# A table of 41 ranks for TensorE's order, and first-tile scores on quarters of the array

## The chip, the core and the metric

The kernel runs on one NeuronCore of a Trainium2 chip. Its time is the device time of one execution in microseconds; a comparison uses the median of several runs. TensorE (PE) multiplies matrices, VectorE (DVE), ScalarE (ACT) and GpSimd (POOL) do the rest, SyncE (SP) issues the transfers. All data are 32-bit floats.

## What is computed

Eight sequences of 512 tokens with 256 features. Each is layer-normalised and goes two ways. One is a causal attention with one head and rotary positions, whose result s is kept. The other is two layers of a local transformer; its output goes through silu and gates s:

```python
xn = _layernorm(x, axis=-1)
s = _L0_attn_ref(xn, w_q, w_k, w_v)          # causal, one head of 256
g = silu(_L0_ffn_ref(xn, ...))               # two layers:
#   h = shift_token(x); q, k, v = split(h @ wqkv)         8 heads of 64
#   q = l2norm(q) * qs; k = l2norm(k) * ksc; rotary_xpos
#   o = softmax over a window of the 128 keys before each query, and itself
#   x = x + o @ wo
#   h = layernorm(shift_token(x)) * lg + lb; h = h @ w1 + b1; a, g = split(h)
#   x = x + (a * gelu(g)) @ w2 + b2
x = x + s * g
```

## The kernel before

The work is cut into 16 slots, one for each sequence b and layer l: (0,0), then (b,0) and (b-1,1) in turn, then (7,1). A slot has four token tiles of 128. For each tile `project` makes q, k and v (TensorE tiles qkv), squares, rotates and scales q and k on ScalarE, VectorE and GpSimd, and `turns` transposes them (qkT). `attend` makes the scores (sps) in two groups of four heads, the softmax, its transposes (pTp, pTr) and the products with the values (ops). `put_out` multiplies with wo (wop), `feed_forward` transposes and normalises (hps, hT), multiplies with w1 (ff) and w2 (w2p), and `finish` transposes back (yps), applies silu, gates and stores (g). `start` loads and normalises a sequence and transposes it (xTp); the causal attention `causal` (inside `start`, tiles qk, v0p, sc, pT0p, av) follows it.

A matmul of 32-bit floats is two passes in the profile, a transpose one. TensorE works in four shapes: the full array; two halves by rows ("rows": the last 42 rows of w2, and the scores of first tiles); two halves by columns ("columns": the values of first tiles); and four quarters of 64 by 64 ("quarters": scores and values of all other tiles). The first tile of a slot has no tile before it, so its window is its own 128 keys. Other tiles have, for each head, scores in a block of 128 columns and one of 64.

The order of TensorE's instructions is made when the program is built. Each job above is a Python generator that yields, before each piece of work, what it needs: a time `at`, events, free buffers and a `rank`. `Order.run` keeps a clock of TensorE, and lets the job with the lowest rank go whose needs are met at that clock; if none can go, the clock moves on. `Order.on` puts the work of the other engines on time lines, and `keep` makes their queues follow the time lines. So each engine's queue is fixed, in order, and a change of one rank can move work of all engines. Ranks before are simple: a slot's number i for attention and transposes, i + 0.1 for projections, i + 1.5 for feed-forward, i - 1.5 for start, -1 for the transposes into feed-forward.

Names in the profile are those of the tiles without numbers; line 223 is the matmul helper, 227 the transpose helper, and 48 the recorder of all other engines. In the text "(7,1) tile 0" is tile 0 of the slot of sequence 7 and layer 1.

Of the kernel before, what the change touches and what calls it, by code (L numbers as in the profile page):

```python
# [14 lines left out]
P = 128  # L15
BATCH = 8
T = 512
NT = T // P
# [4 lines left out]
DH = 64  # L23
# [11 lines left out]

HALF2 = T + 1


# [134 lines left out]
def gated_attention_kernel(  # L173
# [45 lines left out]
    def matmul(out, lhsT, rhs, start, stop, shape="full"):  # L219
        columns = max(out.free_size(), lhsT.free_size())  # L220
        side_by_side = {"full": 1, "rows": 2, "columns": 2, "quarters": 4}[shape]
        order.took(columns * 4 / 2400 / side_by_side * (1.044 if side_by_side == 4 else 1.006), shape)
        nc.tensor.matmul(out, lhsT=lhsT, rhs=rhs, start=start, stop=stop)  # L223
# [156 lines left out]

    def start(b):
# [21 lines left out]
        cos, sin = rope_sb[:, 0], rope_sb[:, 1]  # L405
        yield {"after": [event("started", b)], "free": {"r": 4, "v0": 1}}
        rot = [[buffer("r", [P, T], f"rot_{b}_{n}_{e}") for e in range(2)] for n in range(2)]
        v = buffer("v0", [P, NT, DIM], f"v0_{b}")
        rotated = 0.0
        for n in range(2):  # L410
            even, odd = rot[n]
            for e in range(2):
                yield {"at": arrived[f"wa{n}"], "free": {"bank": 1, "sq": 1 - e, "side": 1 - e}}
                if e == 0:
                    ta, tb = (
                        buffer(tag, [P, T], f"t{a}_{b}_{n}") for tag, a in (("sq", "a"), ("side", "b"))
                    )
                ps = bank(f"qk0_{b}_{n}_{e}")
                for k in range(KC):
                    matmul(  # L420
                        ps,
                        wa[:, n, k, e * P : (e + 1) * P],
                        xT[:, k * HALF2 : k * HALF2 + T],
                        k == 0,
                        k == KC - 1,
                    )
                if e == 0:
                    vector.tensor_mul(even, ps, cos)
                    vector.tensor_mul(tb, ps, sin)
                else:  # L430
                    vector.tensor_mul(ta, ps, sin)
                    vector.tensor_mul(odd, ps, cos)
                at = max(
                    order.on("DVE", 0.69, arrived["rope"], opens=opens)
                    for opens in (("r", "side") if e == 0 else ("sq", "r"))
                )
                free(f"qk0_{b}_{n}_{e}", at)
            gpsimd.tensor_add(even, even, ta)
            gpsimd.tensor_sub(odd, odd, tb)
            rotated = max([rotated] + [order.on("POOL", 1.27, at) for _ in range(2)])  # L440
            for a in "ab":
                free(f"t{a}_{b}_{n}", rotated)
        q, k = rot

        for t2 in range(NT // 2):
            yield {"free": {"bank": 1}}
            ps = bank(f"v0p_{b}_{t2}").rearrange("p (a e) -> p a e", a=2)
# [19 lines left out]
        def scores(t):  # L467
            n = (t + 1) * P
            yield {"at": rotated, "free": {"bank": 1, "p": 1}}
            sps = bank(f"sc0_{b}_{t}")  # L470
# [24 lines left out]
        def turn(t):  # L495
            p, at = ps_p.pop(t)
            yield {"at": at, "free": {"bank": 1, "p": 1}}
            tps = bank(f"pT0p_{b}_{t}").rearrange("p (a b) -> p a b", a=NT)
# [8 lines left out]
        def weigh(t):  # L507
            pT, at = turned.pop(t)
            yield {"at": at, "free": {"bank": 1, "st": 1}}
            av = bank(f"av0_{b}_{t}")  # L510
# [32 lines left out]

    def project(b, l, t, rank):

# [3 lines left out]
        for n in (1, 0, 2):  # L549
            need = {"bank": 1, "v": 1} if n == 2 else {"bank": 1, "r": 1, "sq": 1, "side": 1}  # L550
            yield {"rank": rank, "at": arrived[f"wqkv{l}"], "free": need}
            ps = bank(f"qkv_{nm}_{n}")
# [54 lines left out]
    def turns():  # L607

        for i in range(2 * len(steps)):
# [3 lines left out]
            tag = "kT" if n else "qT"  # L613
            yield {"rank": slots.index((b, l)), "at": at, "free": {"bank": 1, tag: 1}}
            dst = buffer(tag, [P, IC, P], f"{tag}_{nm}")
# [11 lines left out]
    def projections():  # L627

        for i, (b, l, t) in enumerate(steps):
            rank = i // NT + 0.1  # L630
            after = []
            if t == 0:
                after = [event("started", b) if l == 0 else event("fed", b, l - 1, 0)]
            after.append(event("loaded", l))
            if i >= 2:
                after.append(event("attend", *steps[i - 2]))
            yield {"rank": rank, "after": after}
            yield from project(b, l, t, rank)

    def attentions():  # L640
        for i, (b, l) in enumerate(slots):
            yield {"rank": i, "free": {"oT": 1}}
            oT = buffer("oT", [P, IC, T], f"oT_{b}_{l}")
# [5 lines left out]

    def put_out(b, l, part, oT, at, rank):  # L650

# [5 lines left out]
        for m in range(KC):  # L657
            at = max(at, arrived[f"wo{l}"])
            yield {"rank": rank, "at": at, "after": wait, "free": {"bank": 1}}
            name = f"wop_{b}_{l}_{part.start}_{m}"  # L660
# [9 lines left out]

    def attend(b, l, t, oT, rank):

# [15 lines left out]
        for g in range(2):  # L688


            ready = [event("kT", b, l, t), event("qT", b, l, t)]
            yield {"rank": rank, "after": ready, "free": {"bank": 2, "p": 2}}
            done("attend", b, l, t)
            qT, kT, before = qTs[b, l, t], kTs[b, l, t], kTs.get((b, l, t - 1))
            sps = [bank(f"sps_{nm}_{g}_{a}") for a in range(2)]
            for i in range(2):
                c = 2 * g + i
                for a, rows in enumerate(halves):
                    if t == 0:
                        matmul(sps[a][:, main[i]], qT[rows, c], kT[rows, c], True, True, "rows")  # L700
                if t == 0:
                    continue
                for cols, keys in (
                    (main[i], ((before, slice(0, P)), (kT, slice(0, P)))),
                    (rest[i], ((kT, halves[0]), (before, halves[1]))),
                ):
                    for a, rows in enumerate(halves):
                        for queries, (tile_, some) in zip(halves, keys):
                            matmul(
                                sps[a][queries, cols],  # L710
                                qT[rows, c, queries],
# [53 lines left out]
        for g in range(2):  # L765
            at = max(at for key, (_, at) in weighed.items() if key[0] == g)
            need = {"bank": 1 if t == 0 or g else 2}
            yield {"rank": rank, "at": at, "free": need if g else need | {"pT": 1}}
            tps = bank(f"pTp_{nm}_{g}").rearrange("p (h n) -> p h n", h=4)
# [20 lines left out]
        if t > 0:  # L790
# [4 lines left out]
        yield {  # L795
            "rank": rank,
            "at": max(ends) + order.HOP,
# [6 lines left out]
        low, up = halves  # L804
        for c in range(IC):
            heads = [
                (a, slice((2 * c + a) * DH, (2 * c + a + 1) * DH), 4 * (c // 2) + 2 * a + c % 2)
                for a in range(2)
            ]
            if t == 0:  # L810
                for a, h, to in heads:
                    matmul(o_ps[0][halves[a], c, :], v[:, h], pT[:, to, 0:2], True, True, "columns")
                continue

            for a, h, to in heads:
                matmul(o_ps[0][halves[a], c, :], v[low, h], pT[low, to, 1:3], True, False, "quarters")
                matmul(
                    o_ps[1][halves[a], c, :], before[up, h], pT[up, to, 0:2], True, False, "quarters"
                )
            for a, h, to in heads:  # L820
                matmul(
                    o_ps[0][halves[a], c, low], before[low, h], pT[low, to, 0], False, True, "quarters"
                )
                matmul(o_ps[1][halves[a], c, up], v[up, h], pT[up, to, 2], False, True, "quarters")
        free(f"pT_{nm}")
# [16 lines left out]
    def feed_forward(b, l, part, last):  # L842
# [18 lines left out]
        pairs = range(part.start // (2 * P), part.stop // (2 * P))  # L861
        yield {"rank": -1, "after": [event("windowed", b, l, part.start)]}
        yield {"rank": -1, "free": need("hn") | {"tok": len(pairs)}}
        xT = stream[b]
        hn = common("hn", [P, KC, T])
        xh = {t2: buffer("tok", [P, 2, DIM], f"xh_{b}_{l}_{t2}") for t2 in pairs}
        for t2 in pairs:
            yield {"rank": -1, "free": {"bank": 1}}
            hps = bank(f"hps_{b}_{l}_{t2}").rearrange("p (a f) -> p a f", a=2)
# [8 lines left out]
            free(f"hps_{b}_{l}_{t2}", at)  # L878
        yield {"rank": -1, "at": at + order.HOP, "free": {"bank": 2}}
        for c in range(KC):  # L880
# [154 lines left out]
    for i, (b, l) in enumerate(slots):  # L1035
        if l == 0:
            order.add(i - 1.5, start(b))
        parts = parts_of(b, l)
        for n, part in enumerate(parts):
            last = n == len(parts) - 1  # L1040

            order.add(i + 1.5 - n, feed_forward(b, l, part, last))
            if l == DEPTH - 1:
                order.add(i + 2.5 - n, finish(b, part, last))

# [108 lines left out]
```

## Time and profile before

| what | value |
|---|---|
| median of 3 runs | 1457.4 us (1456.26 to 1457.78) |
| profiled execution | 1457.99 us, of which the span 1456.2 us |
| TensorE busy | 1441.5 us (99%) |
| VectorE, ScalarE, GpSimd busy | 936.1, 812.0, 622.6 us |
| granted TensorE clock, mean | 0.998 |
| transfers | 34.25 MB, mean 24 GB/s |

The span is from the first to the last instruction of the profiled execution. A row of the timeline gives a start and a length in microseconds, the engine, the line, the operation, output<-input, the shape and how many instructions were merged; brackets hold the idle time of the engine before it and what ended it. "64*64", "64*128", "128*64" and "128*128" are the part of the array that an instruction uses. Matmuls overlap in the records, so the length of a row is more than the time that it costs.

### The profile page before, as it was taken

To read this page: it belongs to the slowest core of one execution; us is meant where nothing else is said; L and a number is where in the kernel's file an instruction comes from. 1 tells how busy PE (TensorE), PEld (TensorE's weight loads), DVE (VectorE), ACT (ScalarE), POOL (GpSimd) and SP (SyncE) were. 2 spreads that over 40 slices of the span, in tenths; PEclk is the share of its full clock that TensorE was granted. 3 is DMA by queue.
4 is the path that set the end of the run, shared out by engine and by line. 5 is a ranking of instruction groups with operands and counts; after the bars stand their busy time and mean duration, and the time that the engine had idled before them with its cause. 6 is when DMAs were issued, how large, how long until landed. Compare 5 with 4: busy or idle time off the path is not lost.

```text
span 1456.2 us, 28897 instructions
## 1 busy us (share of the span) xinstructions
PE 1441.5 (99%) x11082; PEld 843.7 (58%) x11082; DVE 936.1 (64%) x3001; ACT 812.0 (56%) x2033; POOL 622.6 (43%) x651
## 2 busy tenths in 40 slices
PE   8999999999999999999999999999999999999998
PEld 4665655565655556555566555655556555564566
DVE  6777546675566856767566675665756656666554
ACT  2565636574565735746357463673736647473663
POOL 5476254451544516236352453524535244443600
PEclk9999999999999999999999999999999999999999
DMA  9300000000001000010000100001000100001001
GB/s 313 111 9 2 1 12 5 2 1 2 15 1 45 1 16 15 2 44 1 16 15 2 44 2 15 16 9 37 15 2 16 42 3 1 1 2 45 1 1 59
DMA packets 27418, 34.25 MB, mean 24 GB/s; under 512 B 3176, under 2 KB 23056, under 8 KB 27280
## 3 DMA queue, kind: packets, MB, share of 16 engines
q1 hardware_dynamic: 27280, 32.40, 6.7%
q8 instruction: 88, 1.44, 0.4%
q14 instruction: 50, 0.41, 0.1%
HBM read 24.00 MB, written 8.39 MB: 22 GB/s over the span
## 4 chain that ended last, share of the span: by engine, by line
PE 95%; DVE 2%; ACT 1%; DMA 1%; POOL 1%; issue 0%; SPq 0%; DVEq 0%; POOLq 0%; ACTq 0%
PE qkv L223 22%; PE ff L223 21%; PE w2p L223 11%; PE wop L223 8%; PE ops L223 6%; PE sps L223 6%; PE qkT L227 4%; PE pTp L227 4%; PE qk L223 3%; PE av L223 2%; PE sc L223 2%; PE v0p L223 2%; PE pTr L227 1%; PE hps L227 1%; PE hT L227 1%; ACT p L48 1%
## 5 line engine op out<-in xcount | busy, mean ns | idle before, releaser
L223 PE MATMUL qkv<-wqkv,xT 128*128 128x512 f32 x768 | 359.1, 599 | 0.0
L48 POOL TENSOR_TENSOR r<-r,side 128x512 f32<-128x512 f32 x128 | 163.1, 1274 | 420.9 <-DVE side L48 341.6
L223 PE MATMUL ff<-hn,w 128*128 128x512 f32 (+1 forms) x680 | 289.8, 570 | 0.0
L48 ACT ACTIVATE p<-p,nmx 128x192 f32<-128x192 f32 (+1 forms) x512 | 219.1, 429 | 58.4 <-DVE nmx L48 57.9
L48 POOL TENSOR_TENSOR rn<-ss,neg_half 128x8 f32<-128x8 f32 x128 | 213.1, 1665 | 10.7
L223 PEld LDWEIGHTS qkv<-wqkv,xT 128*128 128x128 f32 x768 | 134.6, 190 | 115.7 <-issue 109.0
L223 PEld LDWEIGHTS ff<-hn,w 128*128 128x128 f32 x680 | 123.7, 190 | 114.9 <-issue 101.9
L223 PE MATMUL w2p<-hid,w 128*128 128x512 f32 (+3 forms) x408 | 160.9, 579 | 0.0
L48 DVE TENSOR_SCALAR p<-p,rden 128x192 f32<-128x192 f32 (+1 forms) x512 | 150.8, 337 | 9.0
L48 DVE CUSTOM_DVE_ANT_0 p<-sps,mask_sb 128x192 f32<-128x192 f32 (+1 forms) x512 | 140.8, 336 | 17.4 <-PE sps L223 17.2
L48 POOL TENSOR_TENSOR r<-r,rn 128x512 f32<-128x512 f32 x128 | 134.3, 1049 | 10.0
L48 DVE SCALAR_TENSOR_TENSOR hid<-ff,vec,hid 128x512 f32<-128x512 f32 (+3 forms) x119 | 85.0, 715 | 73.2 <-PE ff L223 47.1
L48 DVE TENSOR_TENSOR r<-qkv,tables 128x512 f32<-128x512 f32 x128 | 87.7, 685 | 65.0 <-ACT sq L48 64.9
L48 ACT ACT_TABLE_LOAD x99 | 127.0, 1283 | 2.5 <-PEq L1144 0.7
L223 PE MATMUL wop<-oT,wo 128*128 128x512 f32 (+1 forms) x272 | 113.7, 571 | 0.0
L223 PEld LDWEIGHTS w2p<-hid,w 128*128 128x128 f32 (+1 forms) x408 | 68.2, 189 | 77.9 <-issue 74.3
L48 ACT ACTIVATE sq<-qkv 128x512 f32<-128x512 f32 x128 | 75.5, 593 | 64.0 <-PE qkv L223 45.8
L223 PEld LDWEIGHTS ops<-pT,v 64*64 64x64 f32 (+1 forms) x3328 | 82.5, 134 | 37.6 <-issue 26.6
L48 ACT ACTIVATION_READ_ACCUMULATOR p<-p,nmx 128x1 f32 x512 | 95.9, 187 | 0.0
L223 PE MATMUL sps<-kT,qT 64*64 64x64 f32 (+2 forms) x3328 | 94.0, 248 | 0.7 <-ACT qT L48 0.7
L223 PEld LDWEIGHTS sps<-kT,qT 64*64 64x64 f32 (+1 forms) x3328 | 85.0, 138 | 15.2 <-issue 13.1
L48 ACT COPY oT<-ops 128x512 f32<-128x512 f32 x55 | 32.2, 586 | 110.0 <-PE ops L223 110.0
(91 smaller groups left out, 2032.0 us busy)
## 6 DMA issues: line engine op xcount, KB each, us to landing
s<-st SPq DMA_DIRECT2D x32, 128.0 KB, 1.8
again<-s SPq DMA_DIRECT2D x16, 256.0 KB, 3.1
again<-in_x_dram SPq DMA_DIRECT2D x16, 256.0 KB, 3.8
w<-in_w_dram SPq DMA_DIRECT2D x6, 640.0 KB, 9.3
out_dram<-g SPq DMA_DIRECT2D x15, 256.0 KB, 2.3
x<-in_x_dram SPq DMA_DIRECT2D x7, 512.0 KB, 5.2
wqkv<-in_wqkv_dram SPq DMA_DIRECT2D x2, 1536.0 KB, 10.2
tables<-in_xpos_dram SPq DMA_DIRECT2D x2, 512.0 KB, 7.4
```

Source lines behind the costliest of these rows:

```text
L48: ins = getattr(self.engine, name)(*args, **kwargs)
L223: nc.tensor.matmul(out, lhsT=lhsT, rhs=rhs, start=start, stop=stop)
L227: nc.tensor.transpose(out, in_, ident)
```

## The change

A table `SHIFT` of 41 numbers is added, by kind of job and slot (or sequence), and a function that adds its entry to the usual rank. All jobs take their rank from it. The causal attention, which took its rank from `start`, has one of its own, its slot less 1.5. The scores of first tiles, which were on row halves, go on quarters like the others, which makes eight matmuls of a group instead of four, with 64 queries each. In the other tiles, all blocks of 128 columns of a group go first, then all of 64. The loop of the value products is rewritten, and a constant of the clock for quarters changes from 1.044 to 1.04.

```diff
+SHIFT = {
+    "causal": {5: 1.5, 7: 1.5},
+    "finish": {1: 0.75, 4: 1.5, 5: -0.5},
+    "forward": {0: 2, 2: 1.5, 3: 0.25, 4: 1, 5: 1.5, 7: 2, 8: 1, 9: 1, 11: 1, 12: 0.75, 16: 1.5},
+    "out": {14: 1.25},
+    "project": {1: 1.5, 5: -1, 8: -1, 12: -0.75, 15: -0.25},
+    "scores": {1: -0.25, 4: -2, 5: -2.25, 8: -1, 9: -1.5, 12: -1.5, 15: -1},
+    "start": {6: 1.5},
+    "turn": {4: -1, 5: -1.5, 6: 1, 7: -1.5, 8: 2, 10: 0.75, 13: 1, 14: 0.5},
+    "weigh": {3: 1.5, 6: -1, 12: -0.75},
+}
...
-        order.took(columns * 4 / 2400 / side_by_side * (1.044 if side_by_side == 4 else 1.006), shape)
+        order.took(columns * 4 / 2400 / side_by_side * (1.04 if side_by_side == 4 else 1.006), shape)
...
+    def rank(kind, i, usual):
+
+        return usual + SHIFT.get(kind, {}).get(i, 0.0)
...
+        slot = slots.index((b, 0))
+        rest = rank("causal", b, slot - 1.5)
+        yield {"rank": rest, "after": [event("started", b)], "free": {"r": 4, "v0": 1}}
...
-            yield {"rank": rank, "after": ready, "free": {"bank": 2, "p": 2}}
+            yield {"rank": rank("scores", slot, slot), "after": ready, "free": {"bank": 2, "p": 2}}
...
-            for i in range(2):
-                c = 2 * g + i
-                for a, rows in enumerate(halves):
-                    if t == 0:
-                        matmul(sps[a][:, main[i]], qT[rows, c], kT[rows, c], True, True, "rows")
-                if t == 0:
-                    continue
-                for cols, keys in (
-                    (main[i], ((before, slice(0, P)), (kT, slice(0, P)))),
-                    (rest[i], ((kT, halves[0]), (before, halves[1]))),
-                ):
+            whole = slice(0, P)
+            blocks = [(main, ((before or kT, whole), (kT, whole)))]
+            if t > 0:
+                blocks.append((rest, ((kT, halves[0]), (before, halves[1]))))
+            for columns, keys in blocks:
+                for i in range(2):
+                    c = 2 * g + i
                     for a, rows in enumerate(halves):
                         for queries, (tile_, some) in zip(halves, keys):
                             matmul(
-                                sps[a][queries, cols],
+                                sps[a][queries, columns[i]],
...
-            order.add(i - 1.5, start(b))
+            order.add(rank("start", b, i - 1.5), start(b))
...
-            order.add(i + 1.5 - n, feed_forward(b, l, part, last))
+            order.add(rank("forward", i + n, i + 1.5 - n), feed_forward(b, l, part, last))
...
-                order.add(i + 2.5 - n, finish(b, part, last))
+                order.add(rank("finish", b + n, i + 2.5 - n), finish(b, part, last))
```

More of the change, by code (lines that the diff above doesn't have):

```diff
@@ L405, in start @@
         cos, sin = rope_sb[:, 0], rope_sb[:, 1]
-        yield {"after": [event("started", b)], "free": {"r": 4, "v0": 1}}
+        slot = slots.index((b, 0))
+        rest = rank("causal", b, slot - 1.5)
+        yield {"rank": rest, "after": [event("started", b)], "free": {"r": 4, "v0": 1}}
         rot = [[buffer("r", [P, T], f"rot_{b}_{n}_{e}") for e in range(2)] for n in range(2)]
@@ L412, in start @@
             for e in range(2):
-                yield {"at": arrived[f"wa{n}"], "free": {"bank": 1, "sq": 1 - e, "side": 1 - e}}
+                yield {"rank": rest, "at": arrived[f"wa{n}"], "free": {"bank": 1, "sq": 1 - e, "side": 1 - e}}
                 if e == 0:
@@ L445, in start @@
         for t2 in range(NT // 2):
-            yield {"free": {"bank": 1}}
+            yield {"rank": rest, "free": {"bank": 1}}
             ps = bank(f"v0p_{b}_{t2}").rearrange("p (a e) -> p a e", a=2)
@@ L468, in scores @@
             n = (t + 1) * P
-            yield {"at": rotated, "free": {"bank": 1, "p": 1}}
+            yield {"rank": rest, "at": rotated, "free": {"bank": 1, "p": 1}}
             sps = bank(f"sc0_{b}_{t}")
@@ L496, in turn @@
             p, at = ps_p.pop(t)
-            yield {"at": at, "free": {"bank": 1, "p": 1}}
+            yield {"rank": rest, "at": at, "free": {"bank": 1, "p": 1}}
             tps = bank(f"pT0p_{b}_{t}").rearrange("p (a b) -> p a b", a=NT)
@@ L508, in weigh @@
             pT, at = turned.pop(t)
-            yield {"at": at, "free": {"bank": 1, "st": 1}}
+            yield {"rank": rest, "at": at, "free": {"bank": 1, "st": 1}}
             av = bank(f"av0_{b}_{t}")
@@ L542, in gated_attention_kernel, with project @@
     turning = []
-    def project(b, l, t, rank):
+    def project(b, l, t, first):
         wqkv_sb, tables = layers[l][0:2]
@@ L550, in project @@
             need = {"bank": 1, "v": 1} if n == 2 else {"bank": 1, "r": 1, "sq": 1, "side": 1}
-            yield {"rank": rank, "at": arrived[f"wqkv{l}"], "free": need}
+            yield {"rank": first, "at": arrived[f"wqkv{l}"], "free": need}
             ps = bank(f"qkv_{nm}_{n}")
@@ L613, in turns @@
             tag = "kT" if n else "qT"
-            yield {"rank": slots.index((b, l)), "at": at, "free": {"bank": 1, tag: 1}}
+            slot = slots.index((b, l))
+            yield {"rank": rank("turn", slot, slot), "at": at, "free": {"bank": 1, tag: 1}}
             dst = buffer(tag, [P, IC, P], f"{tag}_{nm}")
@@ L629, in projections @@
         for i, (b, l, t) in enumerate(steps):
-            rank = i // NT + 0.1
             after = []
@@ L636, in projections @@
                 after.append(event("attend", *steps[i - 2]))
-            yield {"rank": rank, "after": after}
-            yield from project(b, l, t, rank)
+            first = rank("project", i // NT, i // NT + 0.1)
+            yield {"rank": first, "after": after}
+            yield from project(b, l, t, first)
     def attentions():
         for i, (b, l) in enumerate(slots):
-            yield {"rank": i, "free": {"oT": 1}}
+            yield {"rank": rank("scores", i, i), "free": {"oT": 1}}
             oT = buffer("oT", [P, IC, T], f"oT_{b}_{l}")
@@ L648, in attentions, with put_out @@
             free(f"oT_{b}_{l}")
-    def put_out(b, l, part, oT, at, rank):
+    def put_out(b, l, part, oT, at, slot):
         wo_sb = layers[l][2]
@@ L658, in put_out @@
             at = max(at, arrived[f"wo{l}"])
-            yield {"rank": rank, "at": at, "after": wait, "free": {"bank": 1}}
+            yield {"rank": rank("out", slot, slot), "at": at, "after": wait, "free": {"bank": 1}}
             name = f"wop_{b}_{l}_{part.start}_{m}"
@@ L669, in put_out, with attend @@
         done("windowed", b, l, part.start, at=end)
-    def attend(b, l, t, oT, rank):
+    def attend(b, l, t, oT, slot):
         nm = f"{b}_{l}_{t}"
@@ L767, in attend @@
             need = {"bank": 1 if t == 0 or g else 2}
-            yield {"rank": rank, "at": at, "free": need if g else need | {"pT": 1}}
+            need = need if g else need | {"pT": 1}
+            yield {"rank": rank("weigh", slot, slot), "at": at, "free": need}
             tps = bank(f"pTp_{nm}_{g}").rearrange("p (h n) -> p h n", h=4)
@@ L795, in attend @@
         yield {
-            "rank": rank,
+            "rank": rank("weigh", slot, slot),
             "at": max(ends) + order.HOP,
@@ L804, in attend @@
         low, up = halves
[L805 to L824, printed above, removed]
+        heads = [
+            (c, a, slice((2 * c + a) * DH, (2 * c + a + 1) * DH), 4 * (c // 2) + 2 * a + c % 2)
+            for c in range(IC)
+            for a in range(2)
+        ]
+        if t == 0:
+            for c, a, h, to in heads:
+                matmul(o_ps[0][halves[a], c, :], v[:, h], pT[:, to, 0:2], True, True, "columns")
+        else:
+            for chunk in range(IC):
+                two = heads[2 * chunk : 2 * chunk + 2]
+                for c, a, h, to in two:
+                    for ps, half, tile_, at in ((o_ps[0], low, v, 1), (o_ps[1], up, before, 0)):
+                        columns = pT[half, to, at : at + 2]
+                        matmul(ps[halves[a], c], tile_[half, h], columns, True, False, "quarters")
+                for c, a, h, to in two:
+                    for ps, half, tile_, at in ((o_ps[0], low, before, 0), (o_ps[1], up, v, 2)):
+                        columns = pT[half, to, at]
+                        matmul(ps[halves[a], c, half], tile_[half, h], columns, False, True, "quarters")
         free(f"pT_{nm}")
@@ L861, in feed_forward @@
         pairs = range(part.start // (2 * P), part.stop // (2 * P))
-        yield {"rank": -1, "after": [event("windowed", b, l, part.start)]}
-        yield {"rank": -1, "free": need("hn") | {"tok": len(pairs)}}
+        soon = rank("norm", slots.index((b, l)) + part.start // P, -1)
+        yield {"rank": soon, "after": [event("windowed", b, l, part.start)]}
+        yield {"rank": soon, "free": need("hn") | {"tok": len(pairs)}}
         xT = stream[b]
@@ L867, in feed_forward @@
         for t2 in pairs:
-            yield {"rank": -1, "free": {"bank": 1}}
+            yield {"rank": soon, "free": {"bank": 1}}
             hps = bank(f"hps_{b}_{l}_{t2}").rearrange("p (a f) -> p a f", a=2)
@@ L878, in feed_forward @@
             free(f"hps_{b}_{l}_{t2}", at)
-        yield {"rank": -1, "at": at + order.HOP, "free": {"bank": 2}}
+        yield {"rank": soon, "at": at + order.HOP, "free": {"bank": 2}}
         for c in range(KC):
```

## The prediction

> **What bounds the kernel now.** I read the page's busy table and its chain first, then the windows by stretch, then TensorE's timeline.
>
> ```profile
> PE 1441.5 (99%) x11082; PEld 843.7 (58%) x11082; DVE 936.1 (64%) x3001; ACT 812.0 (56%) x2033; POOL 622.6 (43%) x651
> PE 95%; DVE 2%; ACT 1%; DMA 1%; POOL 1%; issue 0%; SPq 0%; DVEq 0%; POOLq 0%; ACTq 0%
> ```
>
> TensorE is busy 99% of the span and holds 95% of the chain; no other engine passes 64%. So only three things can pay: less TensorE time for the same work, fewer waits of TensorE, a shorter tail behind it. "Busy" hides the first, since pipelined matmuls overlap in the records. I therefore take the difference between the starts of successive rows of TensorE's timeline (columns: start, length, instruction, count):
>
> ```profile
> 623.03 4.46 PE L223 MATMUL w2p<-hid,w 128*128 128x512 f32 x10
> 627.41 1.57 PE L223 MATMUL ops<-pT,v 64*64 64x128 f32 x64
> 628.91 5.62 PE L223 MATMUL w2p<-hid,w 128*128 128x512 f32 x14
> 634.46 7.13 PE L223 MATMUL wop<-oT,wo 128*128 128x512 f32 x16
> ...
> 643.30 1.16 PE L223 MATMUL sps<-kT,qT 64*128 64x128 f32 x16
> 644.39 5.42 PE L223 MATMUL qkv<-wqkv,xT 128*128 128x512 f32 x12
> ...
> 656.64 1.09 PE L223 MATMUL ops<-pT,v 128*64 128x128 f32 x16
> 657.66 1.98 PE L223 MATMUL qkv<-wqkv,xT 128*128 128x512 f32 x4
> 659.48 0.60 PE L227 MATMUL qkT<-ident,r 128*128 128x128 f32 x4
> 659.92 3.60 PE L223 MATMUL qkv<-wqkv,xT 128*128 128x512 f32 x8
> 663.35 0.60 PE L227 MATMUL qkT<-ident,r 128*128 128x128 f32 x4
> ```
>
> Eight undisturbed passes take 663.35 - 659.92 = 3.43 us, 0.429 each; four transposes 0.44, 0.109 each. Ten passes ahead of the small tiles take 627.41 - 623.03 = 4.38, so leaving the full array costs 4.38 - 4.29 = 0.09. Four passes after small tiles take 659.48 - 657.66 = 1.82 against 1.72: coming back costs 0.10 (0.06 when transposes come first: eight hT transposes between two half scores, 131.03 to 132.06, take 1.03 = 0.87 + 0.09 + 0.06). The small stretches themselves, start to start: values on quarters 1.50, first-tile scores on row halves 1.09, first-tile values on column halves 1.02. Other rows give scores on quarters 1.50 (667.32 to 668.82), half of them 0.83 (132.06 to 132.88), half a first tile's 0.64 (568.43 to 569.07). The x14 row holds four row-half passes: 5.55 - 4.29 - 0.19 = 1.06. Two small stretches in a row:
>
> ```profile
> 232.61 1.09 PE L223 MATMUL ops<-pT,v 128*64 128x128 f32 x16
> ...
> 235.14 1.98 PE L223 MATMUL qkv<-wqkv,xT 128*128 128x512 f32 x4
> ...
> 702.15 1.57 PE L223 MATMUL ops<-pT,v 64*64 64x128 f32 x64
> ...
> 704.99 4.56 PE L223 MATMUL w2p<-hid,w 128*128 128x512 f32 x10
> ```
>
> Values and scores together take 2.84, not 3.00; column values and scores 2.53, as 1.02 + 1.50. One excursion from the full array less also saves 0.09 + 0.10.
>
> The waits lie at two places. By the windows TensorE idles 4.9 us in 0 to 100, 0.14 in 100 to 1300, 3.3 in 1300 to 1366, and it ends 6.3 us before the span does. The last slot, from 1311.65 to 1359.22, takes 47.57 us; its work by the cadences above is 72 passes (30.9), 52 transposes (5.7), 2.56 and 1.09 of small tiles, 0.3 of changes: 40.6. So 7.0 us are lost there, the most of it here:
>
> ```profile
> 1350.09 1.88 PE L223 MATMUL qkv<-wqkv,xT 128*128 128x512 f32 x4
> 1353.98 1.11 PE L227 MATMUL pTp<-ident,p 128*128 128x128 f32 x4 [2.01 <-DVE p L48]
> ```
>
> and, from VectorE's timeline and from the windows,
>
> ```profile
> 1352.61 0.69 DVE L48 TENSOR_TENSOR r<-qkv,tables 128x512 f32<-128x512 f32 x1 [3.59 <-ACT sq L48]
> ```
> ```profile
> 1355.00:1356.00 1.00, 1.00 (x3) 0.70 0.00 0
> 1356.00:1357.00 1.00, 1.00 (x2) 0.50 0.03 8
> ```
>
> TensorE waits 2.01 us for the weights of (7,1) tile 0. They wait in VectorE's queue behind r<-qkv, which waits 3.59 us for a square that ScalarE runs behind two hn (1.42 us). Then the granted clock (third number of the last two rows) falls to 0.70, 0.50, 0.50, 0.59 for four windows of 1 us: 0.30 + 0.50 + 0.50 + 0.41 = 1.7 us more. [...] The trace shows 2.0 + 1.7 = 3.7 and decides.
>
> **The change, part by part.**
>
> *Fewer changes of shape.* Counted in the order of both programs, TensorE leaves the full array 119 times before and 102 after. First instruction on return: a matmul 89 then 65, a transpose 30 then 37. Exits 17 x 0.09 = 1.5, returns 24 x 0.10 - 7 x 0.06 = 2.0: 3.5 us. The stretches, as change in count by duration: values+scores +4 x 2.84, values alone -2 x 1.50, scores alone -11 x 1.50, half scores -3 x 0.83, column values alone -9 x 1.02, column values+scores +6 x 2.53, row-half w2p alone -2 x 1.06, with values -1 x 2.56, with column values and scores +3 x 3.59, values+half scores -1 x 2.17, first-tile scores on rows -15 x 1.09 and -2 x 0.64, on quarters +16 x 1.05. Sum -1.5 us. Part: 5.0, said as 5.1 with unrounded changes.
>
> *First tiles on quarters.* 1.05 is an estimate: half scores hold 3072 columns (0.83), whole ones 6144 (1.50), this has 4096: 0.83 + 0.67/3. It doubles the passes, 16 more per tile, 256 in all. [...] In the trace 32 further passes cost 0.67 us, 21 ns each with all their columns, since four run side by side. I take the row[...].
>
> *128-column chunks in one go.* The same instructions with the 64-column ones after instead of between. The trace of before has no such row; quarters with both sizes take 0.67 per 3072 columns against 0.64 of array time, so at most 0.03 per 32 passes, 96 x 0.03 = 2.9 us, either way. I take 0: the number of quarter passes in flight is the same. The values loop is only rewritten; its sequence on TensorE is the same.
>
> *The last slot.* In the new order the weights of (7,1) tile 0 are turned 6.2 us (12 qkv passes, 8 hps) after their scores, not 4.8; VectorE runs both rden and the scaling ahead of r<-qkv; ScalarE runs hn after the exps and the squares. The scores of (7,1) tile 0 no longer stand right behind their qT (0.72 us wait before), and pTp of (6,1) tile 3 comes 9.9 us after its scores instead of 2.7 (1.2 us lost before). What is late next: ff of (6,1) stands right behind hT, whose first hn (773 ns) it needs: about 0.7, with the other half of ff and the last qkv of (7,1) queued behind it, whose readers have slack; value products of (7,1) tile 0 come 1.0 us behind their transposes: 0.3; qT of tile 1: 0.3; hT itself behind VectorE: 0.3; 0.2 elsewhere. 7.0 - 1.8 = 5.2. Ends: 7.0 if nothing waits, 1.5 if one 3.7 us wait returns.
>
> *The tail.* Before, the store of g (7,0), 256 KB, is the last: issued 1453.16, lands in 2.1. After, yps (7,0) stands ahead of the last w2p, and g (7,3), 128 KB, is last: issued 1451.83 in this trace, lands in 1.9 or less. 1.33 + 0.2 = 1.5, less 0.43 for four transposes that ran in the shadow of the last add: 1.1.
>
> *The middle.* TensorE's order is the same, apart from the shape of one score tile, to the start of the next projection at 89.4, so the start's losses stay. From there some distances get shorter than any that before ran without a wait: av of (3,0) tiles 0 and 1 come 0.44 us behind their transposes (shortest before 0.78), ops of (3,0) tile 0 0.6 us behind (copy alone 589 ns), qkT of (2,0) 5.8 us behind its projection (6.9): 0.3 + 0.3 + 0.4 + 0.5 = 1.5 against 0.7 lost there before: 0.8 lost. Queues: 25 copies go from VectorE (692 ns) to ScalarE (589 ns), three more table loads (1283 ns): 18.6 us on an engine 56% busy, hidden behind TensorE's other work. SyncE issues the same 119 transfers; s of batches 5 and 6, x 6 and 7 come later in its row. With a DMA share of 0.04 in the middle I take 0; if the cover is gone, one x load (5.2 us to land) is what TensorE waits for.
>
> Sum: 5.1 + 5.2 + 1.1 - 0.8 = 10.6 us. The profiled execution took 1457.99 for a span of 1456.2, 0.6 above the median of the three runs, 1457.4. Span 1445.6, execution 1447.4, median 1446.8.
>
> **Rivals.** *Only the shapes and the tail pay:* waits move to other places as large. For it: the order was found on the kernel's own time lines, which missed the 3.59 us wait; against: the new queues visibly mend that place. 1457.4 - 6.2 = 1451.2. [...] *Slower:* VectorE's queue again holds weights behind a projection whose square is late, now in the middle, where each batch has its own ranks; price 2.0 + 1.7 = 3.7 each. Three such waits eat the gain, four give 1446.8 + 14.8 = 1461.6. Against it: 0.14 us idle in 1200 us before. *The order doesn't move:* out, all rows of TensorE's sequence after 89 us differ.
>
> **How the numbers follow.** Forecast 0.63, shapes and tail alone 0.22, overhead 0.06 (all three faster by over 0.2%), two or three of the late waits 0.04, four or more 0.05. Range 1442 (no waits in the last slot or middle, chunks paying) to 1453 (rivals one and two). 0.2% is 2.9 us, about what a measurement of this kernel can tell from no change: faster 0.91, same 0.04, slower 0.05.
>
> **What would show it.** Right: first-tile scores as x32 rows of about 1.05 us; (7,1) without a wait near 2 us or a clock of 0.50; 102 excursions; TensorE's last row to the end about 4.8 us instead of 6.3; the middle still at 0.1 to 1 us idle. Wrong: first-tile stretches of 1.2 or more, or new waits of TensorE over 1 us between 100 and 1300.

## The result, and the profile after

| | before | after |
|---|---|---|
| median of 6 runs | 1457.24 us (1456.26 to 1457.78) | 1448.0 us (1447.89 to 1448.61) |
| profiled execution, and its span | 1457.99, 1456.2 | 1448.0, 1446.2 |
| mean clock | 0.998 | 0.999 |

The ratio is 0.9939 (95% interval 0.9926 to 0.9952): faster by 9.2 us, where 10.6 were forecast (1446.8).

The page after, its busy row and its chain by engine:

```profile
PE 1433.3 (99%) x11338; PEld 841.9 (58%) x11338; DVE 913.7 (63%) x2976; ACT 825.0 (57%) x2061; POOL 626.4 (43%) x651
PE 94%; DVE 2%; ACT 2%; POOL 1%; DMA 1%; issue 0%; SPq 0%; POOLq 0%; ACTq 0%
```

TensorE still bounds the kernel. Its busy time fell by 8.2 us although it runs 256 more instructions. The windows (stretch, length and busy time, clock, DMA share, GB/s) show that idle time has moved:

```profile
100.00:1300.00 1200.00, 1197.39 (x9597) 1.00 0.04 14
1300.00:1366.00 66.00, 65.50 (x500) 1.00 0.00 1
```

In 100 to 1300 TensorE now idles 2.6 us (0.14 before), in 1300 to 1366 only 0.5 (3.3 before), and the clock stays at 1.00 there. The wait that the forecast hung on has not gone everywhere; it is back at another place:

```profile
1085.06 1.05 ACT L63 ACTIVATE sq<-qkv 128x512 f32<-128x512 f32 x2
...
1085.67 0.69 DVE L63 TENSOR_TENSOR r<-qkv,tables 128x512 f32<-128x512 f32 x1 [3.65 <-ACT sq L63]
1086.27 0.15 DVE L63 RECIPROCAL rden<-den 128x2 f32<-128x2 f32 x1
1086.46 0.48 DVE L63 TENSOR_SCALAR p<-p,rden 128x128 f32<-128x128 f32 x2
...
1080.57 5.42 PE L238 MATMUL qkv<-wqkv,xT 128*128 128x512 f32 x12
1086.90 1.03 PE L242 MATMUL pTp<-ident,p 128*128 128x128 f32 x4 [0.91 <-DVE p L63]
```

This is the wait of (7,1) in the profile before, now at (5,1): VectorE stands 3.65 us at r<-qkv for ScalarE's square. rden and the scaling of p are queued behind it, though the exponentials that they need ended between 1082 and 1085, and TensorE waits for p. The bracket on the PE row counts 0.91 us; by starts, twelve passes and the return to the full array need 5.15 + 0.10, so the transposes come 1086.90 - 1080.57 - 5.25 = 1.08 late. Then they run only as fast as VectorE scales p: the next row starts at 1087.76, 0.86 behind them, where four transposes need 0.44. In all 1.5 us are lost. A bracket shows only the idle time ahead of a row's first instruction.

I sum all such losses from starts: the distance of two rows less the cadences of the prediction (0.429 per pass, 0.109 per transpose, 0.09, 0.10 and 0.06 for changes of shape). What is above 0.02 us is a wait; the rest, with what small tiles take, is TensorE's work. In us:

| profiled execution | to the first transpose | work | waits, 0 to 80 | waits, middle | waits, last slot (from 1295) and end | start of the last transpose to the end | span |
|---|---|---|---|---|---|---|---|
| before | 6.72 | 1428.64 | 5.78 | 1.02 | 7.44 | 6.59 | 1456.2 |
| after | 6.55 | 1422.77 | 5.69 | 4.73 | 1.65 | 4.82 | 1446.2 |
| no_shift | 6.15 | 1427.67 | 5.76 | 1.00 | 7.47 | 6.60 | 1454.6 |
| first_rows | 6.71 | 1423.70 | 5.04 | 4.59 | 1.64 | 4.82 | 1446.5 |
| mixed_chunks | 6.72 | 1422.80 | 5.95 | 4.70 | 1.65 | 4.82 | 1446.6 |
| last_only | 6.20 | 1426.50 | 5.90 | 5.06 | 5.39 | 4.81 | 1453.9 |
| not_last | 6.14 | 1426.54 | 8.21 | 4.80 | 1.97 | 6.60 | 1454.3 |
| late_r | 6.72 | 1422.68 | 5.69 | 2.06 | 1.39 | 4.83 | 1443.4 |
| before_late_r | 6.08 | 1428.60 | 4.68 | 1.02 | 3.08 | 6.60 | 1450.1 |

The last slot after:

```profile
1340.17 1.10 PE L238 MATMUL sps<-kT,qT 64*64 64x128 f32 x32
1341.20 1.09 PE L242 MATMUL hps<-ident,xT 128*128 128x128 f32 x8
1342.13 5.32 PE L238 MATMUL qkv<-wqkv,xT 128*128 128x512 f32 x12
1347.29 1.04 PE L242 MATMUL pTp<-ident,p 128*128 128x128 f32 x8
...
1351.65 1.09 PE L242 MATMUL hT<-ident,xh 128*128 128x128 f32 x8
1353.17 3.70 PE L238 MATMUL ff<-hn,w 128*128 128x512 f32 x8 [0.43 <-ACT hn L63]
```

The first-tile scores on quarters take 1341.20 - 1340.17 = 1.03 us, and the weights pTp of (7,1) follow 12 projection passes later without a wait. ff comes 1353.17 - 1351.65 = 1.52 us after hT, whose eight transposes and return take 0.93. That is 0.59 lost; the eight passes of ff take 0.11 more than their cadence (1356.71 - 1353.17 = 3.54 against 3.43), so 0.70 go here, as forecast.

### The profile page after: what moved, and what is told of

Same layout as the page of the kernel before. It is cut to its first block, busy times and chain, and to the rows that moved or that the text cites. A ratio compares the mean times of both kernels' runs of the same rounds, so it can differ in the third digit from the quotient of the medians.

```text
span 1446.2 us, 29500 instructions
## 1 busy us (share of the span) xinstructions
PE 1433.3 (99%) x11338; PEld 841.9 (58%) x11338; DVE 913.7 (63%) x2976; ACT 825.0 (57%) x2061; POOL 626.4 (43%) x651
## 4 chain that ended last, share of the span: by engine, by line
PE 94%; DVE 2%; ACT 2%; POOL 1%; DMA 1%; issue 0%; SPq 0%; POOLq 0%; ACTq 0%
PE qkv L238 21%; PE ff L238 21%; PE w2p L238 11%; PE wop L238 8%; PE ops L238 6%; PE sps L238 5%; PE qkT L242 4%; PE pTp L242 4%; PE qk L238 3%; PE av L238 2%; PE sc L238 2%; PE v0p L238 2%; PE pTr L242 1%; PE hps L242 1%; PE hT L242 1%; ACT p L63 1%
## 5 line engine op out<-in xcount | busy, mean ns | idle before, releaser
L238 PE MATMUL qkv<-wqkv,xT 128*128 128x512 f32 x768 | 352.8, 598 | 0.0
L63 DVE TENSOR_SCALAR p<-p,rden 128x192 f32<-128x192 f32 (+1 forms) x512 | 141.9, 320 | 8.6
L63 DVE TENSOR_TENSOR r<-qkv,tables 128x512 f32<-128x512 f32 x128 | 87.6, 684 | 63.5 <-ACT sq L63 63.5
L63 ACT ACTIVATE hid<-ff,vec 128x512 f32<-128x512 f32 (+2 forms) x102 | 67.3, 662 | 65.0 <-PE ff L238 63.3
L63 ACT COPY pT<-pTp 128x512 f32<-128x512 f32 x117 | 67.8, 588 | 62.0 <-PE pTp L242 61.6
L242 PEld LDWEIGHTS pTp<-ident,p 128*128 128x128 f32 x512 | 65.4, 141 | 48.3 <-issue 25.0
```

The costliest lines, as they stand in the source:

```text
L63: ins = getattr(self.engine, name)(*args, **kwargs)
L242: nc.tensor.transpose(out, in_, ident)
```

## The experiments

Each was timed beside the kernel before, in 5 to 21 executions.

**Which part of the change carries it.** no_shift is the kernel after with no table:

```diff
-SHIFT = { ... 41 entries ... }
+SHIFT = {}
```

> The changed kernel with an empty table of ranks: what stays of the change is the first tiles' scores on quarters and the 128-column chunks in one go. The queues of all engines are those of the kernel before; only the passes of the score tiles differ. Theory (the table makes the gain, the quarters a little): 15 stretches at 1.03 instead of 1.09 us and two halves at 0.62 instead of 0.64 give 0.9 us less TensorE work: 1456.3, with the waits of the kernel before where they were (about 7 us lost in the last slot). [...] Rival (a good part of the 5.6 us of saved shape time is the quarters'): 1453 to 1455.

Measured: 1456.39 us, before 1456.36; ratio 0.9995 (0.9987 to 1.0004). In the table of sums work falls by 0.97 us and every wait stays. The medians don't show that 0.97, and the clock accounts for it. The old wait is there, and behind it, in the windows of no_shift, the clock halves:

```profile
1352.00:1353.00 1.00, 0.43 (x2) 1.00 0.00 0
1353.00:1354.00 1.00, 0.99 (x3) 0.74 0.00 0
1354.00:1355.00 1.00, 1.00 (x3) 0.50 0.00 0
1355.00:1356.00 1.00, 1.00 (x3) 0.50 0.03 8
1356.00:1357.00 1.00, 1.00 (x4) 0.55 0.00 0
```

But perhaps not in every execution. Those of before on this chip lie in two groups, by their mean clock: eight at 0.998 (median 1457.55) and nine at 0.999 (1456.17). Those of no_shift are seven at 0.998 (1456.81) and six at 0.999 (1455.22). Within a group no_shift is 0.7 and 0.95 us faster, as its work says; a median over two groups depends on which of them happens to hold more executions.

first_rows is the kernel after, with first-tile scores on row halves again (table and chunks kept):

```diff
+                        if t == 0:
+                            for _ in halves:
+                                order.took(P * 4 / 2400 / 4 * 1.04, "quarters")
+                            nc.tensor.matmul(
+                                sps[a][:, columns[i]], lhsT=qT[rows, c], rhs=kT[rows, c], start=True, stop=True
+                            )
+                            continue
```

> The changed kernel with the first tiles' scores back on row halves; the clock that makes the order still counts them as quarters, so that all queues stay as in the changed kernel. Theory (quarters save only the difference of the stretches): 16 x (1.09 - 1.03) = 0.9 us more: 1448.9. Rival (row halves also cost the neighbours, as a third kind of shape): 1450 or more. [...]

Measured: 1448.82 us, ratio 0.9944 (0.9932 to 0.9957). The median lies 0.8 us above after's, too little to tell by itself; in the profile its work is 0.93 us above after's. The rows of its timeline that answer to the first two of the last slot above:

```profile
1340.40 1.16 PE L729 MATMUL sps<-kT,qT 64*128 64x128 f32 x16
1341.49 1.09 PE L242 MATMUL hps<-ident,xT 128*128 128x128 f32 x8
```

1.09 us against 1.03, at 16 first tiles: 0.06 x 16 = 0.96. Twice as many instructions cost nothing here, and quarters gain a little.

mixed_chunks is the kernel after, with chunks of 128 and 64 columns in turn, as before:

```diff
-            for columns, keys in blocks:
-                for i in range(2):
+            for i in range(2):
+                for columns, keys in blocks:
```

> The changed kernel with the scores' 64-column blocks between the 128-column blocks again, as before; nothing else differs, and all queues stay the same. Theory (the order of the chunks costs nothing): 1448.0, scores alone on quarters still 1.50 us for 64 passes, within 0.3. Rival (each change between 128 and 64 columns costs up to 30 ns per 32 passes): up to 1450.9.

Measured: 1448.37 us, ratio 0.9941 (0.9928 to 0.9953); work 1422.80 against 1422.77, 0.03 us over all score stretches of the kernel. The order of the chunks is worth nothing.

So the table carries all but about 1 us.

**Do the table's entries add up?** I split it. last_only keeps the 12 entries of the last slots, not_last the other 29 (both texts of expectation miscount them):

```diff
 # last_only
+    "causal": {7: 1.5}, "finish": {5: -0.5}, "forward": {12: 0.75, 16: 1.5}, "out": {14: 1.25},
+    "project": {12: -0.75, 15: -0.25}, "scores": {12: -1.5, 15: -1},
+    "turn": {13: 1, 14: 0.5}, "weigh": {12: -0.75},
 # not_last: all other entries
```

> The changed kernel with only the 15 entries of the table for slots from 12 on (and causal 7, finish 5); quarters and chunks stay. The queues are those of the kernel before up to about 1080 us. Theory (parts add up): 2.6 us of shapes by the count of stretches, about 6 us of waits in the last slot and 1.3 of the tail, no new waits in the middle: 1457.2 - 9.9 = 1447.3, not slower than the changed kernel although 26 entries are gone. Rival (the middle's entries carry most of the gain): 1452 to 1454.

Measured: 1456.0 us, ratio 0.9991 (0.9984 to 0.9997). A miss. The tail came (4.81), and 2.1 us of work; but the last slot kept 5.39 us of waits and the middle got 5.06. The largest are 2.16 from 1098 to 1111 (yps, qkT), 1.96 from 1280 to 1289 (hT, qkT, ff), 1.56 from 1354 and 2.30 at 1312, where transposes of (6,1) stand only four passes behind their scores:

```profile
1309.66 1.52 PE L237 MATMUL sps<-kT,qT 64*64 64x128 f32 x64
1311.12 1.97 PE L237 MATMUL ff<-hn,tail 128*106 128x512 f32 x4
1313.91 0.56 PE L241 MATMUL pTp<-ident,p 128*128 128x128 f32 x2 [0.83 <-DVE p L62]
```

> The changed kernel with only the 26 entries for the slots below 12 (and sequences below 7, finish 1 and 4); quarters and chunks stay. Theory (parts add up): 3.1 us of shapes, 3.5 us of new waits in the middle and the old waits and tail at the end: 1457.2 - 3.1 + 3.0 = 1457, about the kernel before. Rival (the middle's entries carry most of the gain): 1450 to 1452.

Measured: 1454.2 us, ratio 0.9978 (0.9969 to 0.9988). Also a miss, to the other side: its last slot has 1.97 us of waits, nearly as few as the kernel after, without any of the entries made for it. The tail is the old one, 6.60. (The profiled execution, at 1456.08 the slowest of ten, halved its clock once in the start, which is in its 8.21 us:)

```profile
19.00:20.00 1.00, 0.38 (x2) 1.00 1.10 379
20.00:21.00 1.00, 0.24 (x1) 1.00 1.03 398
21.00:22.00 1.00, 1.00 (x5) 0.71 1.08 379
22.00:23.00 1.00, 1.00 (x5) 0.50 1.06 371
```

By medians the parts gain 1.3 and 3.1 us, the whole 9.2. Most executions of both parts have a clock of 0.999 or more; against those of before at 0.999 (1456.2) the parts gain 0.2 and 2.0 us, the whole 8.2. Either way the parts don't add up, and neither does TensorE's work: beyond the 0.97 of the quarters the table saves 4.9 us of it, the parts 1.2 and 1.1. My theory that the late entries mend the last slot falls: an entry moves all that comes later, so what a late entry does depends on where the earlier ones leave the work. Only the tail belongs to the late entries (4.81 and 4.82 with them, 6.60 without).

**Is it the square that r waits for?** The planner puts r and side on VectorE's time line as if they needed the projection alone. The trace has them wait for the square. late_r leaves TensorE's order and all plans as they are, and only sorts VectorE's queue so that no r or side stands ahead of the planned end of its square (54 instructions change place):

```diff
+            if engine == "DVE":
+                busy.sort(key=lambda b: max(b[0], self.later.get(b[3].name, 0.0)))
...
             squared = order.on("ACT", 0.59, opens="sq")
...
+            late_r = vector.traced[0].name
             order.on("DVE", 0.68, scaled_at[l], opens="r")
+            order.later[late_r] = squared
...
+            late_side = vector.traced[0].name
             rotated = order.on("DVE", 0.68, scaled_at[l], opens="side")
+            order.later[late_side] = squared
```

> The changed kernel with one change in VectorE's queue: r<-qkv and side<-qkv are sorted in not ahead of the planned end of the square that they wait for on ScalarE. TensorE's, ScalarE's, GpSimd's and SyncE's queues are the same as in the changed kernel; 54 places of VectorE's differ. Theory (the waits that replaced the old ones in the middle are weights held behind r<-qkv in VectorE's queue): the waits of pTp at 236 us (0.64 us lost) and 1085 us (1.50 lost) go, the 0.4 to 0.9 us at 297, 315, 469 and 476 stay: 1448.0 - 2.1 = 1445.9. Rival (TensorE waits there because ScalarE and VectorE have too much to do): 1448.0. Rival (r, now later, makes its own transposes late, so that the waits move to qkT): 1448 to 1450, with waits of qkT on GpSimd's r.

Measured: 1444.06 us (1443.89 to 1445.19), ratio 0.9913 (0.9899 to 0.9926): the fastest version. The timeline of late_r at the place of the 1.5 us wait:

```profile
1081.78 0.17 DVE L63 RECIPROCAL rden<-den 128x2 f32<-128x2 f32 x1 [0.86 <-ACT p L63]
1081.98 0.48 DVE L63 TENSOR_SCALAR p<-p,rden 128x128 f32<-128x128 f32 x2
...
1084.29 0.29 DVE L63 TENSOR_SCALAR p<-p,rden 128x128 f32<-128x128 f32 x1
1084.57 0.69 DVE L63 TENSOR_TENSOR r<-qkv,tables 128x512 f32<-128x512 f32 x1
...
1079.47 5.42 PE L241 MATMUL qkv<-wqkv,xT 128*128 128x512 f32 x12
1084.72 0.60 PE L245 MATMUL pTp<-ident,p 128*128 128x128 f32 x4
```

VectorE scales p during the time that it used to stand still, r goes without a wait, and the transposes follow the projection directly: 1084.72 - 1079.47 = 5.25 us, just the twelve passes (5.15) and the return (0.10). The waits at 236, 646 and 1085 are gone (0.64, 0.11, 1.50), and two others with them (0.43 at 476, 0.26 at 1363). The waits fall by 2.9 us in the profile, more than expected; the medians differ by 3.9 (mixed_chunks, which has after's queues, ran on the same chip as late_r, at 1448.37). The profiled execution of late_r is the slowest of its five, 1.1 above their median, and where the others gain is not in a trace.

before_late_r is the same edit on the kernel before (26 instructions change place):

> The kernel before with the same sorting of VectorE's queue (r<-qkv and side<-qkv not ahead of the planned end of their square); TensorE's and all other queues as before, 26 places of VectorE's differ. Theory (the 2.0 us wait at 1352 us is the queue's order, and the halved clock follows from it): the wait of pTp of (7,1) tile 0 goes, and with it the clock of 0.5 and the waits right behind it: 2.0 + 0.5 + 1.7 = 4.2 less: 1453.0; no window at 0.50 after 1350. Rival (the wait is the exps' own length on ScalarE): 1457.2. Rival (the clock falls for another reason): 1455, with windows of 0.50 still there.

Measured: 1452.38 us (1451.87 to 1452.79), ratio 0.9963 (0.9949 to 0.9977), all executions at clock 0.999. The timeline of before_late_r where before waited 2.01 us, and two of its windows (busy time of PE, PEld, DVE, ACT and POOL, then the clock, 1.00 in each from 1346 to 1355):

```profile
1348.28 1.88 PE L226 MATMUL qkv<-wqkv,xT 128*128 128x512 f32 x4
1350.00 0.60 PE L230 MATMUL pTp<-ident,p 128*128 128x128 f32 x4
```
```profile
1350.00:1351.00 1.00, 1.00 (x7) 0.76 (x6) 0.96 (x6) 1.00 (x3) 0.96 (x1) 1.00 0.00 0
1353.00:1354.00 1.00, 1.00 (x6) 0.52 (x4) 1.00 (x3) 0.98 (x3) 0.92 (x3) 1.00 0.00 0
```

The 4.84 us lost around this wait before became 0.48, the clock included. By medians the edit gains 4.9 us, against the executions of before at clock 0.999 it gains 3.8. So about half of what the change gains can be had with one queue put right and TensorE's order left alone.

Not every such wait costs time, though. VectorE waits at r for a square all through both kernels (us in all, times, longest):

```profile
DVE r L48 <- ACT sq L48: 64.9, 47, 5.3
DVE r L63 <- ACT sq L63: 63.5, 37, 6.2
```

The first row is the kernel before, the second the kernel after. Three waits of before last 5.33 us (at 759, 937 and 1116) and hold TensorE up nowhere. What costs time is a p behind r that TensorE needs next: found at one place before (1352) and at three after.

## Why the prediction was right, and which terms were off

The time, 1448.0, lies 1.2 us above the forecast 1446.8 and within the range. By its own steps:

- *Fewer changes of shape, with first tiles on quarters*: 5.1 forecast, 1428.64 - 1422.77 = 5.9 measured. The estimate for a first tile, 1.05, was 1.03, which is 0.3 us over 16 tiles. The other 0.5 isn't placed.
- *The rival "overhead"*: it let quarters cost more than row halves, since they take 256 more instructions. No run shows such a price, and the upper end of my range, 1453, hung on it alone. first_rows shows a gain of 0.93 us for quarters. The row was the right choice: on four quarters side by side, 32 instructions took 1.03 us where 16 on halves took 1.09. Nothing is left of that rival here.
- *Chunks in one go*: 0 forecast, 0.03 measured. (The 0.64 us of array time for 3072 columns is an estimate from the cadence: a quarter of them is 768, one and a half passes of 512, at 0.429 each. Likewise a quarter pass of 96 columns would take 0.080 alone; the 0.021 measured is about a quarter of that.)
- *The last slot*: 5.2 forecast, measured 7.18 - 0.96 = 6.2 (without the last yps). Of what I let be late next, ff behind hT came (0.70 for 0.7), and one turn of q (0.26 for 0.3, of tile 2 and not 1); the other 0.8 did not. That the wait and its clock went together is shown by before_late_r.
- *The tail*: 1.1 forecast; 6.59 - 4.82, less 0.43 more at the last yps (0.69 for 0.26), is 1.3. From TensorE's end, as the prediction counted, it is 6.32 and now 4.54 us to the end of the span.
- *The middle*: -0.8 forecast, measured 1.02 - 4.73 = -3.7. **This is the term that failed.** "From there some distances get shorter than any that before ran without a wait" was the right test and its places were right: qkT of (2,0) 0.88 (0.5), av of (3,0) 0.62 (0.3 a tile), ops of (3,0) 0.36 (0.4). But I applied it to TensorE's distances alone. I did not look for r in VectorE's new queue ahead of p, the mechanism that I named for the rival "slower". It came back at 236, 646 and 1085 and cost 2.25 us there, most of the 2.9 by which this term is off.
- *The rival "slower"*: right in mechanism and place, too dear in price. "Price 2.0 + 1.7 = 3.7 each": the waits cost 0.11, 0.64 and 1.50, and the clock kept 1.00 behind all of them. The rival "waits move to other places as large" was true in part: 6.2 us of waits went from the last slot, 3.7 came in the middle, so the sum kept a gain.
- *From the sum to the median*: I took 0.6 off because the profiled execution of before was 0.6 above its median. That 0.6 was one side of before's two groups (below). The kernel after keeps the full clock in its profile from 6.38 us to TensorE's last instruction at 1441.67, its six executions lie within 0.7 us, and its profile lies at its median. That was half of the miss: 0.6 here, and 10.6 - 10.0 in the sum, since 5.9 + 6.2 + 1.3 - 3.7 and 0.3 at the start give 10.0. That the sum came so near is in part luck: shapes, last slot, tail and start brought 2.3 us more than I forecast, and the middle took 2.9 more.

The rows of the tail, SyncE's last store among them:

```profile
1438.75 0.48 DVE L63 SCALAR_TENSOR_TENSOR yT<-w2p,vec,xT 128x256 f32<-128x256 f32 x1
1440.38 0.27 PE L242 MATMUL yps<-ident,yT 128*128 128x128 f32 x1
1440.58 0.48 DVE L63 SCALAR_TENSOR_TENSOR yT<-w2p,vec,xT 128x256 f32<-128x256 f32 x1 [1.36 <-PE w2p L238]
1441.12 0.55 PE L242 MATMUL yps<-ident,yT 128*128 128x128 f32 x3 [0.47 <-DVE yT L63]
...
out_dram<-g SPq DMA_DIRECT2D x2, 128.0 KB, 1.7
```

The second yT waits for the last w2p, and the remaining transposes for it, now with nothing between; the last store is the half one, 1.7 us to landing.

Of TensorE's waits in the kernel after, those of the middle, by what TensorE waited for (us in all, times, longest):

```profile
PE pTp L242 <- DVE p L63: 0.9, 1, 0.9
PE qkT L242 <- POOL r L63: 0.9, 2, 0.7
PE av L238 <- ACT pT L63: 0.3, 1, 0.3
PE ops L238 <- ACT pT L63: 0.3, 1, 0.3
```

In late_r the first is gone and the second is 0.7, once. What stays is short distances of TensorE's own order, which the table could still lengthen; I did not try that.

## What to carry to other kernels

When a planner fixes all queues, check its dependencies against the brackets of the trace first: an instruction that really waits for another engine, planned as if it didn't, blocks whatever is queued behind it (here r, for 3.65 us, and behind it the p that TensorE needed), and an order made on such a plan can move the wait instead of removing it. Where a prediction names a queue as the cause of a wait, look for the same pair of instructions in the whole new queue, not only at the old place, and count only those with something behind them that the bounding engine needs next. And before medians a microsecond apart are compared, see whether the executions lie in groups by their granted clock (here near 1456.2 and 1457.6 us, at 0.999 and 0.998).

## What the runs showed of the hardware that I had not expected

By their mean clocks, the executions of one kernel fall into groups. On the two chips of the experiments, 23 of 47 executions of before stand at 0.999 and 22 at 0.998, with medians near 1456.2 and 1457.6, and two at 0.997 above 1460. The 1.4 us between the groups is near the 1.7 that the profile charges to the clock; that the halving sits at this wait is known only for the profiled ones, but before_late_r, without the wait, has none of its five at 0.998.

The clock records of the traces show when the clock changes. In before full clock begins at 7.14 us, falls to 0.50 at 1355.41, is back at 1358.82 and falls again at 1454.39, which is 4.51 us after TensorE's last instruction. The distances, 1348.27, 3.41 and 95.57 us, are 395, 1 and 28 times 3.4133. In after full clock lasts from 6.38 to 1443.39, 421 times that. The second fall of before is in this window:

```profile
1454.00:1455.00 1.00, 0.00 (x0) 0.70 0.74 262
```

TensorE stands still here, and the clock's mean of 0.70 is that of the prediction's window at 1355: both falls lie at about the same fraction of a microsecond, 98.99 us or 29 times 3.4133 apart. What sets these distances, and whether they have to do with the groups of executions, the runs do not show.

In the 3.41 us ahead of the falls TensorE had no instruction for 2.05 us in before, 2.17 in no_shift and 1.38 in the start of not_last. After other stretches of this length the clock stayed at 1.00: with 1.17 us idle in before (17.38 to 20.80) and 1.24 in after (23.45 to 26.86). Whether idle time alone decides it stays open.

VectorE's read of a projection waited for ScalarE's read of the same tile, though neither writes it: in the kernel after, r starts 0.03 us after the first square ends (1085.63, 1085.67), and so it does at the end of all 37 waits of r (63.5 us) there. The trace shows this order; it does not show what would happen without.
